# Two transformer layers on one core: where the second pass adds its third operand, and when five pieces of side work run

## The chip, the cores and the metric

The kernel runs on one core of a Trainium2 chip. A core has five engines, each with its own queue of instructions that it works off in order: TensorE (PE in the profile; its weight loads are PEld), VectorE (DVE), ScalarE (ACT), GpSimd (POOL) and SyncE (SP), which here only issues transfers. POOL and ACT issue transfers too. Sixteen DMA engines carry them all. The metric is the time of one execution on the device, in microseconds (us); lower is better.

## The reference, cut to what matters

The input is 8 sequences of 256 tokens with 512 features, in fp32. The reference runs two layers.

```python
x = x + L0_attn(layernorm(x)) + L0_ffn(layernorm(x))
x = x + L1_attn(layernorm(x)) + L1_ffn(layernorm(x))
```

`L0_attn` has 32 heads of 128. It takes queries, keys and values as `silu(xn @ qkv_w.T)`, weighs query-key scores with a decay instead of a softmax, multiplies them with the values, normalises over all heads, multiplies with `sigmoid(xn @ gate_w.T)` and projects back to 512 features. `L0_ffn` is a mixture of 16 experts, of which each token takes two, and a shared expert:

```python
y = y + ge[:, None] * ((silu(xt @ w1 + b1) * (xt @ w2 + b2)) @ w3 + b3)
```

`L1_attn` is one head of softmax attention of width 128. `L1_ffn` holds 64 pairs of low-rank factors, of which each token takes 16 by a softmax over its best scores:

```python
h = einsum("nd,krd->nkr", x, A); out = einsum("nkr,kdr->nd", h * G[:, :, None], B) * 2
```

## The kernel before, in words

**Tokens and stages.** The 2048 tokens are four chunks of 512. An opening (to about 130 us) normalises them, routes them to experts and runs the shared expert. Then come two passes over the heads of the first layer: the first takes chunks 0 and 1 together, the second chunks 2 and 3. Then the second layer takes the chunks one after another, 0 to 3 (from about 2420 us).

**Seven products for eight.** Large matrix products are made by a scheme that replaces eight half-size products by seven and some additions of halves, and this twice, one inside the other. A pass is 8 groups of four heads, each in two halves (`h`: first queries and keys, then gates and values), so 16 halves a pass, numbered through as `at`, 0 to 31 (16 to 31 are the second pass). A half is seven *outer* products (class `Outer`, L1177), in the order p1 p2 p6 p5 p3 p7 p4. In the first pass the sums of weight halves that they need are made on VectorE and GpSimd and stored; the second pass loads them.

An outer product is again seven *inner* products, each a few matmuls into a bank of 512 columns, in the order p1, p7, p3 of the outer product before, p6, p4, p2, p5. Three banks are read in between, while TensorE goes on: p1 fills bank `a` and it is copied to `c1`; p7 fills bank `e`, copied to `c3`; p6 adds onto `a`, copied to `c2`. The copies are ScalarE's (`copied`, L1199; the instruction is listed at L1201). TensorE may not add onto a bank until its copy is done: p6 waits for `c1`, p5 for `c2`, p4 for `c3`. Each of the four quarters of the result is a bank plus such a copy (`result`, L1204), an add on VectorE. What the outer scheme still wants is a third operand: the quarter of an earlier outer product (tile `a` or `c`), added by GpSimd in a second instruction, either in place (p2, p5, p3) or through a tile `r` (p6, p4, p7). One quarter, (0,1), takes no copy.

**The order of the rest.** Within the two passes the order on ScalarE, GpSimd and VectorE is that in which the program issues the instructions. After each inner product, `slot` (L881) takes the side work that is due, one counted piece at a time (two when more than twelve wait): `later(n, f)` (L877) makes `f` due n slots on. A half has 49 slots. Side work is:

- the attention of the head pairs and its results `gT`; `output` (L1039) makes from four of them the seven operands of the output projection, with adds and subtractions on GpSimd, and puts off each `project` (L1065) by some slots: p7 by 6;
- 36 expert tiles in the halves 17 to 27 (`expert`, L1296): two gathers on GpSimd's queue fetch tokens and weights into one of two large buffers, `staged`; 10 slots later the tokens are turned, 12 slots later a third gather puts the output bias where the tokens were (`bias`, L916), at 14 comes the first product, at 19 the second (`down`, L940), whose VectorE add reads that bias (`ye`);
- `low_sums` (L1351) for the two low-rank factors, in half 28 at slots 16 and 48: it loads quarters of a factor into the two `staged` buffers by SyncE, makes sums on GpSimd and stores them;
- `settle_early` (L1399), in half 29 at slot 34: loads chunk 1, gathers its two expert rows a token (`gather`, L614, eight gathers on GpSimd's queue), adds them times their gates (`settle`, L624, eight VectorE instructions), and stores the chunk;
- `wrapped_up` (L1405), in half 30 at slot 26: the same for chunk 0, and its normalisation. Both take the `staged` buffers as well.

**The second layer.** For each chunk, `seven` (L1533) runs three times: twice over the first low-rank factor (`low_rank`, banks times gates that are spread by DMA, `spread_g`) and once over the second. Lists of functions, `fill1` and `fill2`, are called after the named inner product. The operands of the second factor come by `load_fb` (L1600), called after p5 of the first `seven` of chunk 0. At the start of a chunk the next one is loaded (`next_x`); from chunk 1 on its expert rows are gathered into two `spare` buffers and settled inside the fills. Chunk 1 itself was settled before. Outside the two passes a scheduler arranges the order from these calls.

Of the kernel before, what the change touches and what calls it, by code (L numbers as in the profile page):

```python
# [24 lines left out]
NB = 2  # L25
# [4 lines left out]
NG = H // HG  # L30
# [43 lines left out]
def block_kernel(  # L74
# [721 lines left out]
    with tc.tile_pool(name="attn", bufs=1) as attn, tc.manual_schedule(engines={mybir.EngineType.Activation, mybir.EngineType.Pool, mybir.EngineType.DVE}):  # L796
# [232 lines left out]
        class Unit:  # L1029
# [9 lines left out]
            def output(self, l, t, pair, gT):  # L1039
# [7 lines left out]
                elif (t, pair) == (1, 0):  # L1047
                    O[l, "p7"] = self.gated()
                    sub(O[l, "p7"], A[l, 0, 0], gT, pool)
                    ready = (("p7", 6),)  # L1050
                elif (t, pair) == (1, 1):
                    O[l, "p4"] = gT
                    O[l, "p5"], O[l, "p6"] = A[l, 1, 0], A[l, 0, 0]
                    add(A[l, 1, 0], A[l, 1, 0], gT, pool)
                    sub(A[l, 0, 0], A[l, 1, 0], A[l, 0, 0], pool)
                    ready = (("p4", 3), ("p5", 7), ("p6", 10))
                else:
                    O[l, "p2"] = gT
                    O[l, "p3"] = A[l, 1, 1]
                    sub(A[l, 1, 1], gT, O[l, "p6"], pool)  # L1060
                    ready = (("p2", 4), ("p3", 7))
# [115 lines left out]
        class Outer:  # L1177
# [20 lines left out]

            def copied(self, bank):  # L1199
                c = attn.tile([P, 512], FP, tag="cp", name="cp", bufs=5)  # L1200
                nc.scalar.copy(c, bank)  # L1201
                return c

            def result(self, i, j, bank, c):  # L1204
# [7 lines left out]
                if made:  # L1212
# [5 lines left out]
                    else:  # L1218
                        add(o, bank, c)
                        if with_:  # L1220
                            add(o, o, u.tile(self.h, with_)[:, q], pool)
                elif c is None and p != "p7":
                    add(a, bank, a)
                else:
# [22 lines left out]
            def p1(self):  # L1247
                self.a = ps_a()
                self.go(self.a, "p1", True)
                self.c1 = self.copied(self.a)  # L1250
                self.after("p1")

            def p7(self):
                self.e = ps_e()
                self.go(self.e, "p7", True)
                self.c3 = self.copied(self.e)
                self.after("p7")

            def p6(self):
                self.go(self.a, "p6")  # L1260
                self.c2 = self.copied(self.a)
                self.after("p6")
# [33 lines left out]
        def expert(j):  # L1296
# [3 lines left out]
            later(14, e.up)  # L1300
            later(19, e.down)

# [95 lines left out]

        def settle_early():  # L1399

            x_, y = spare8(), spare8()
            settled_in(1, x_, y)
            later(41, lambda: nc.sync.dma_start(out=xs_[1], in_=x_))

        def wrapped_up():  # L1405
# [73 lines left out]
        for n, (i, g, h, p) in enumerate(plan):  # L1479
# [4 lines left out]
            if k == 0:  # L1484
# [12 lines left out]
                if at == 2 * NB * NG - 4:  # L1497
                    later(16, partial(low_sums, 0))
                    later(48, partial(low_sums, 1))
                if at == 2 * NB * NG - 2:  # L1500
                    later(26, wrapped_up)
                if at == 2 * NB * NG - 3:
                    later(34, settle_early)
            if h == 0 and k in (0, 2):
# [110 lines left out]
    for i in range(NCH):  # L1615
# [85 lines left out]
        if i + 1 < NCH:  # L1701
            following = [next_x(i + 1)]
            if i:
                following += [spare(), spare()]
                for n in range(TOP):
                    gather(i + 1, n, following[1 + n])
        fill1 = {
# [5 lines left out]
        if following:  # L1713
# [9 lines left out]
            if i:  # L1723
                fill1[1].append(lambda: finish(i + 1, following[0], kept=tc.keep_in_program_order))
            for n, fill, k, ts in () if i == 0 else (
                (0, fill1, 5, (0, 1)), (0, fill1, 3, (2, 3)), (1, fill1, 4, (0, 1)), (1, fill2, 2, (2, 3)),
            ):
# [5 lines left out]
        if i == 0:  # L1733
            fill1[5].append(load_fb)
        low_rank(0, fill1)
# [133 lines left out]
```

## Time and profile before

| what | value |
|---|---|
| median of 3 runs | 2734.82 us (2734.21 to 2735.54) |
| the profiled execution | 2731.75 us, span 2730.0 us |
| TensorE matmul busy | 2647.9 us (97%) |
| VectorE busy | 1759.5 us (64%) |
| GpSimd busy | 1655.1 us (61%) |
| ScalarE busy | 966.8 us (35%) |
| mean granted TensorE clock | 0.987 |

The span runs from the first instruction to the last. A matmul row is counted as busy while its columns stream, so a busy TensorE also includes time at a lower granted clock (PEclk, 1.00 is full speed). A line of waits reads: engine, tile and line that waited, what ended the wait, total us, how often, the longest. A line of the timeline reads: start, duration, engine, line, operation, output and inputs, form, how many were merged, and in brackets the idle time before it and what ended it. A line of windows gives a stretch, its length, and for each engine busy us and instructions, then PEclk, the busy share of the DMA engines and GB/s.

### The profile page before, as it was taken

How to read it: one execution, taken by the hardware profiler on the slowest of the kernel's cores; microseconds unless marked ns; L12 is line 12 of the kernel's file. 1: busy time of each engine (PE TensorE's matmuls, PEld its weight loads, DVE VectorE, ACT ScalarE, POOL GpSimd, SP SyncE). 2: the span in 40 equal slices, each digit the busy share in tenths (PEclk: the TensorE clock that was granted, in tenths of full speed). 3: DMA queues.
4: the chain of work that ended last, by engine and by line, in shares of the span. 5: the costliest groups of instructions: out<-in, count | busy, mean ns of one | idle time of the engine just before them, and what ended most of it. 6: DMA issues, size and time to landing. Idle time of an engine off the chain costs nothing. (4 is left out here: it accounts for less than half of the span.)

```text
span 2730.0 us, 39198 instructions
## 1 busy us (share of the span) xinstructions
PE 2647.9 (97%) x14218; PEld 2303.0 (84%) x14218; DVE 1759.5 (64%) x2985; ACT 966.8 (35%) x1455; POOL 1655.1 (61%) x1502
## 2 busy tenths in 40 slices
PE   8999999999999999999999999999999989999999
PEld 5488989898989898988889898888889878877777
DVE  8697777777778787856445454555555545756664
ACT  4234343433333334343434242333334232421121
POOL 7468686867686767667646556575746675662210
PEclk9999999999999999999999999999999999999999
DMA  6897777776777786867767676767677695632211
GB/s 247 305 380 284 262 263 274 256 284 244 284 256 284 264 287 239 300 250 272 251 231 279 226 273 222 278 229 271 248 247 260 233 336 197 225 98 104 80 49 64
DMA packets 163411, 657.74 MB, mean 241 GB/s; under 512 B 19808, under 2 KB 22368, under 8 KB 160992
## 3 DMA queue, kind: packets, MB, share of 16 engines
q1 hardware_dynamic: 126224, 501.26, 52.3%
q10 hardware_dynamic: 21024, 92.81, 8.4%
q0 software_dynamic: 15968, 61.13, 6.9%
q8 instruction: 115, 1.88, 0.3%
q14 instruction: 80, 0.66, 0.1%
HBM read 513.18 MB, written 144.83 MB: 241 GB/s over the span
## 5 line engine op out<-in xcount | busy, mean ns | idle before, releaser
L872 PE MATMUL ps_a<-xt,w 128*128 128x256 f32 x2688 | 720.9, 383 | 13.4 <-DMA xt<-xc 4.0
L1201 ACT COPY cp<-ps_a 128x512 f32<-128x512 f32 x448 | 261.5, 584 | 914.6 <-PE ps_a L872 820.8
L103 POOL TENSOR_TENSOR c<-c 128x512 f32<-128x512 f32 x288 | 374.0, 1311 | 332.5 <-DVE c L103 321.6
L103 POOL TENSOR_TENSOR c<-c,r 128x512 f32<-128x512 f32 x320 | 431.1, 1363 | 196.4 <-DVE r L103 178.9
L872 PEld LDWEIGHTS ps_a<-xt,w 128*128 128x128 f32 x2688 | 474.8, 193 | 69.6 <-issue 16.1
L1069 PE MATMUL ps_sc<-wo,gT 128*128 128x256 f32 x1792 | 427.1, 382 | 12.4 <-POOL gT L103 12.1
L1069 PEld LDWEIGHTS ps_sc<-wo,gT 128*128 128x128 f32 x1792 | 335.9, 191 | 58.0 <-POOL gT L103 13.6
L872 PE MATMUL ps_e<-xt,w 128*128 128x256 f32 x1344 | 369.9, 385 | 11.2 <-DVE c L103 9.6
L103 DVE TENSOR_TENSOR w<-w 128x256 f32<-128x256 f32 (+1 forms) x464 | 329.7, 720 | 9.0 <-DMA w<-in_w_att_dram 3.6
L103 POOL TENSOR_TENSOR sums<-sums,sq 128x256 f32<-128x256 f32 x240 | 193.3, 805 | 165.5 <-ACT sq L1007 155.9
L872 PEld LDWEIGHTS ps_a<-w,xt 128*128 128x128 f32 x1792 | 271.7, 192 | 23.5
L872 PE MATMUL ps_a<-w,xt 128*128 128x128 f32 x1792 | 273.2, 275 | 0.0
L872 PEld LDWEIGHTS ps_e<-xt,w 128*128 128x128 f32 x1344 | 234.4, 193 | 37.1 <-DVE c L103 11.7
L103 DVE TENSOR_TENSOR acc<-ps_sc,acc 128x512 f32<-128x512 f32 x196 | 134.9, 688 | 188.4 <-PE ps_sc L1069 188.2
L1016 DVE SCALAR_TENSOR_TENSOR gT<-ps_o,nw,c 128x256 f32<-128x256 f32 x256 | 111.9, 478 | 206.7 <-ACT sq L1007 202.4
L1201 ACT COPY cp<-ps_e 128x512 f32<-128x512 f32 x224 | 131.2, 586 | 192.1 <-PE ps_e L872 188.2
L103 DVE TENSOR_TENSOR s<-ps_sc,decay 128x384 f32<-128x384 f32 x256 | 139.6, 551 | 78.9 <-PE ps_sc L984 77.8
L872 PE MATMUL ps_b<-xt,w 128*128 128x256 f32 x672 | 182.1, 380 | 0.0
L103 DVE TENSOR_TENSOR c<-ps_a,c 128x512 f32<-128x512 f32 x160 | 109.9, 687 | 102.9 <-PE ps_a L872 101.3
L103 DVE TENSOR_TENSOR c<-c,r 128x512 f32<-128x512 f32 x128 | 174.7, 1395 | 0.1
L103 POOL TENSOR_TENSOR gT<-gT 128x512 f32<-128x512 f32 x128 | 166.7, 1302 | 2.9 <-DVE gT L1016 0.4
L996 PE MATMUL ps_o<-s,c 128*128 128x256 f32 x512 | 156.7, 388 | 7.2 <-DVE gT L1016 6.3
(289 smaller groups left out, 4208.9 us busy)
## 6 DMA issues: line engine op xcount, KB each, us to landing
xt<-xc SPq DMA_DIRECT2D x224, 896.0 KB
w<-in_w_att_dram SPq DMA_DIRECT2D x144, 512.0 KB
w<-in_w_att_dram SPq DMA_DIRECT2D x48, 384.0 KB
wo<-in_w_out_dram SPq DMA_DIRECT2D x56, 256.0 KB
decay<-dec SPq DMA_DIRECT2D x32, 384.0 KB
yd<-ye SPq DMA_DIRECT2D x36, 256.0 KB
wos<-wo ACTq DMA_DIRECT2D x32, 256.0 KB
wo<-wos SPq DMA_DIRECT2D x32, 256.0 KB
```

What stands on the lines that cost most here:

```text
L103: (eng or nc.vector).tensor_tensor(o, a, b, op)
L872: mm(o, a, b, start=(first and ty == 0), stop=True, skip_group_check=True)
L996: mm(po[:, bass.ts(hh, S)], v[:, 0:P], s[:, 0:S], start=True, stop=False)
L1016: nc.vector.scalar_tensor_tensor(gT[:, h, :], po[:, bass.ts(h, S)], nw[:, n : n + 1], self.c[:, 2 * h + t, 0:S], ALU.mult, ALU.mult,)
L1069: mm(py[:, bass.ts(t, S)], self.O[l, p][:, hh, bass.ts(t, P)], self.wo[p][:, hh, :], start=(t == 0 and hh == 0), stop=(hh == 1), skip_grou ...
L1201: nc.scalar.copy(c, bank)
```

## The change

In the second pass, thirteen of the copies of a half's outer products (all three of p2, p6, p5 and p3, and `c2` of p4) become a VectorE add of the bank and the third operand. The later add of bank and `c` then yields the whole result, and GpSimd's add is left out. Five pieces of side work move: the projection p7 from 6 to 8 slots (both passes), `down` from 19 to 24, the second `low_sums` from slot 48 to 57; `settle_early` is gone, and chunk 1 is gathered and settled in the second layer, in the fills of chunk 0; `load_fb` is called after p2 of the second `seven` instead of after p5 of the first. The calls that settle in the fills move by some products in all chunks.

```diff
-                    ready = (("p7", 6),)
+                    ready = (("p7", 8),)
...
-            def copied(self, bank):
+            def folded(self, q):
+
+                return self.u.i and (self.p, q) not in (("p4", 0), ("p4", 3)) and {"p2": "a", "p5": "a", "p6": "a", "p4": "a", "p3": "c"}.get(self.p)
+
+            def copied(self, bank, q):
                 c = attn.tile([P, 512], FP, tag="cp", name="cp", bufs=5)
-                nc.scalar.copy(c, bank)
+                with_ = self.folded(q)
+                if with_:
+                    add(c, bank, self.u.tile(self.h, with_)[:, q])
+                else:
+                    nc.scalar.copy(c, bank)
                 return c
...
                         add(o, bank, c)
-                        if with_:
+                        if with_ and not self.folded(q):
                             add(o, o, u.tile(self.h, with_)[:, q], pool)
-                elif c is None and p != "p7":
-                    add(a, bank, a)
+                elif p != "p7" and (c is None or self.folded(q)):
+                    add(a, bank, a if c is None else c)
                 else:
...
-                self.c1 = self.copied(self.a)
+                self.c1 = self.copied(self.a, 0)
...
-            later(19, e.down)
+            later(24, e.down)
...
-        def settle_early():
-
-            x_, y = spare8(), spare8()
-            settled_in(1, x_, y)
-            later(41, lambda: nc.sync.dma_start(out=xs_[1], in_=x_))
...
-                    later(48, partial(low_sums, 1))
+                    later(57, partial(low_sums, 1))
...
-                if at == 2 * NB * NG - 3:
-                    later(34, settle_early)
...
-            following = [next_x(i + 1)]
-            if i:
-                following += [spare(), spare()]
-                for n in range(TOP):
-                    gather(i + 1, n, following[1 + n])
+            following = [next_x(i + 1), spare(), spare()]
+            for n in range(TOP):
+                gather(i + 1, n, following[1 + n])
...
-            for n, fill, k, ts in () if i == 0 else (
-                (0, fill1, 5, (0, 1)), (0, fill1, 3, (2, 3)), (1, fill1, 4, (0, 1)), (1, fill2, 2, (2, 3)),
+            for n, fill, k, ts in (
+                (0, fill1, 3, (0, 1)), (0, fill1, 4, (2, 3)), (1, fill2, 2, (0, 1)), (1, fill2, 7, (2, 3)),
             ):
...
         if i == 0:
-            fill1[5].append(load_fb)
+            fill2[2].append(load_fb)
```

More of the change, by code (lines that the diff above doesn't have):

```diff
@@ L1255, in p7 @@
                 self.go(self.e, "p7", True)
-                self.c3 = self.copied(self.e)
+                self.c3 = self.copied(self.e, 3)
                 self.after("p7")
@@ L1260, in p6 @@
                 self.go(self.a, "p6")
-                self.c2 = self.copied(self.a)
+                self.c2 = self.copied(self.a, 2)
                 self.after("p6")
```

## The prediction

> **What bounds the kernel now.** I read the page first: TensorE is busy 97% of the span, so only its remaining idle time, and time at a lowered clock, can be won. I then asked who TensorE waited for, by stage, then for the clock around each long wait, and last for the timeline ahead of them, to see what held the engine that was late.
>
> Waits of TensorE, first pass (130 to 1230 us) and second (1230 to 2420):
>
> ```profile
> PE ps_sc L1069 <- POOL gT L103: 12.1, 8, 2.2
> ...
> PE ps_e L872 <- DVE c L103: 9.6, 3, 3.4
> PE ps_o L996 <- DVE gT L1016: 5.4, 1, 5.4
> PE ps_sc L983 <- ACT c L960: 4.7, 3, 3.1
> PE ps_a L872 <- DMA xt<-xc: 4.0, 1, 4.0
> PE ps_a L872 <- DVE c L103: 2.8, 1, 2.8
> PE ps_a L872 <- DVE r L103: 2.2, 2, 1.2
> ```
>
> Few and long waits, not many short ones. Windows of 15 us around five of the longest and around one at 630 us:
>
> ```profile
> 1390.00:1405.00 15.00, 11.64 (x48) 9.63 (x48) 5.25 (x8) 3.66 (x5) 7.88 (x7) 0.77 0.67 230
> 1550.00:1565.00 15.00, 11.82 (x57) 10.07 (x56) 6.46 (x11) 4.02 (x6) 9.23 (x9) 0.89 0.76 265
> 2192.00:2207.00 15.00, 10.97 (x56) 9.87 (x55) 4.08 (x7) 3.34 (x5) 11.45 (x11) 0.77 1.02 393
> 2244.00:2259.00 15.00, 9.57 (x38) 8.17 (x37) 6.35 (x9) 8.83 (x11) 12.26 (x12) 0.77 0.44 161
> 2312.00:2327.00 15.00, 11.77 (x44) 9.26 (x43) 9.58 (x11) 4.36 (x7) 13.08 (x11) 0.77 0.89 333
> 625.00:640.00 15.00, 12.83 (x72) 11.33 (x72) 11.23 (x16) 4.72 (x7) 11.32 (x11) 0.89 0.68 222
> ```
>
> The third column from the end is PEclk: each long wait is followed by a stretch at lowered clock that costs (1 - 0.77) x 15 = 3.45 us or (1 - 0.89) x 15 = 1.65 us more. What comes before the wait at 1395, and before that at 2198 (timeline):
>
> ```profile
> 1387.37 1.02 POOL L918 DMA_INDIRECT xw<-in_b_dram,own__1114  x1 [0.16 <-PE ps_a L872]
> 1394.38 0.69 DVE L103 TENSOR_TENSOR ye<-ps_sc,xw 128x512 f32<-128x512 f32 x1 [6.46 <-DMA xw<-in_b_dram,own__1114]
> 1395.73 2.07 PE L872 MATMUL ps_e<-xt,w 128*128 128x256 f32 x4 [3.36 <-DVE c L103]
> ...
> 2181.66 8.00 SPq L1364 DMA_DIRECT2D low<-in_fb_dram  x3
> ```
>
> The bias of an expert is fetched at 1387.37 and VectorE stands 6.46 us at the add that reads it; the banks queue behind. SyncE stands 8.00 us at the second factor's loads, until the first factor's buffers are stored, and TensorE then lacks tokens for 4.0 us.
>
> **The change, part by part.**
>
> *p7 two slots later.* All eight waits of 12.1 us are p7's operand, made by GpSimd, in the first pass. In the built order the projection now stands behind two more inner products, which start 0.88 us apart there: 1.76 us of cover. The four waits of 2.15 to 2.19 us keep 0.4 each, the rest go; the lowered clock at 630 us (1.65) goes too. 12.1 - 1.6 + 1.65 = **-12.1**. The seven `gT` buffers are held two products longer; no wait of the trace is for one of them, so I charge nothing. If the cover fails, 12.1 stays.
>
> *`down` five slots later.* The waits of 9.6 us (1395, 1554, 1712) all follow a `ye` that stood 6.2 to 6.5 us for its bias. Five slots are at least 5 x 0.86 (the spacing of inner products in the other halves) = 4.3 us and with the slots' own matmuls more like 7; GpSimd, rid of its adds, also fetches sooner. **-9.6 - 3.45 - 1.65 - 1.65 = -16.35.** Late next: in the three halves with four experts the gather for the second next expert stands ahead of `down` in the built order and now waits on GpSimd's queue for that `ye`, a slot or two; behind it stand the next bias (eleven slots of cover) and sums. Nothing for it in the sum.
>
> *Second factor nine slots later.* Nine slots are over 7.7 us, and SyncE stood 8.00; GpSimd reaches the stores sooner. **-4.0 - 3.45 = -7.45.**
>
> *Chunk 1 leaves the second pass.* At 2250 TensorE waits 5.4 us for `gT`, after GpSimd did four gathers and the adds queued behind them, on which ScalarE's gates (7.87 us) and the queue behind hung. At 2316 GpSimd had stood 6.9 us for the store of `settle_early`'s buffer before `wrapped_up` could gather. Both causes go: **-5.4 - 3.45 - 2.8 - 3.45 = -15.1.** Two 1 MB loads or stores on SyncE's queue and eight gathers (1.05 us each) go with it.
>
> *Third operand on VectorE.* 16 halves x 13 = 208 copies (ScalarE, 584 ns) become VectorE adds. The new form (bank and tile) has its row: c<-ps_a,c, 689 ns. So VectorE gets 208 x 0.689 = 143 us: 636 of 1190 us busy becomes 779 (65%). GpSimd loses 208 adds of 1.28 to 1.33 us, some 270 of 728 us. These rows of the second pass carry it:
>
> ```profile
> L103 DVE TENSOR_TENSOR c<-c,r 128x512 f32<-128x512 f32 x64 | 87.4, 1397 | 0.1
> L103 DVE TENSOR_TENSOR c<-ps_a,c 128x512 f32<-128x512 f32 x78 | 53.8, 689 | 64.4 <-PE ps_a L872 62.8
> L103 POOL TENSOR_TENSOR c<-c 128x512 f32<-128x512 f32 x141 | 178.3, 1280 | 188.5 <-DVE c L103 185.5 <-DVE rms L244 2.4
> ```
>
> Gained: silu and gate no longer wait for GpSimd to finish a tile, so the 4.7 us before L983 go, with the clock after the first (1.65): **-6.35**. Paid: TensorE needs a copied bank again two inner products later. At 0.86 us each that is 1.7 us, against 0.69 plus some 0.25 to hand over. What matters is whether VectorE is free. I laid the 208 adds into its queue in the timeline, each behind what the program issues before it: seven in ten start as the bank is ready, and all but 16 end before TensorE needs the bank. The 16 are late by 20.1 us together; 8.6 of that are two places (1252, 2171) where VectorE sits in c<-c,r rows of up to 5.4 us while GpSimd runs the adds that go. From 0 to +20; I take **+8**, near the 11.5 left without those two.
>
> *Layer 2, chunk 0.* Eight VectorE settles (0.74 us in the quiet rows, 1.12 in the second pass: 6 to 9 us) and eight gathers come in. GpSimd runs the gathers ahead of four bias adds, which end near 2460 instead of 2452.6; VectorE wants the first at 2463.7, so that hides. The gathers move 2.1 MB while the DMA engines are full (2450 to 2465, 254 to 399 GB/s): 6.7 us more ahead of the first `spread_g`, on which VectorE already stood 7.5 and 3.3 us and TensorE 2.2. In the other direction, in SyncE's built order the first transfer of the second factor stays put, and its other four (2.1 MB) now follow the second `spread_g`, on which VectorE stood 5.2 us and TensorE later 1.8 and 4.2. Ends: +6.7 and a lowered clock, and two microseconds for the settles, +12; or -6. I take **+4**, since the settles must end before the statistics that TensorE's 4.2 us hang on.
>
> *Moved settles of chunks 2 and 3*: TensorE has only 1.4 and 0.75 us waits there; nothing.
>
> Sum: -12.1 - 16.35 - 7.45 - 15.1 - 6.35 + 8 + 4 = **-45.4**. Against the profiled execution, 2731.75, that is 2686.4; that execution was 3.1 us under the median 2734.8, so on the median **2689**.
>
> A rule weighed against the rows: the Trainium skill (TensorE: Matmul & The Clock Gate, Part 1) lets the clock fall after an idle window of some 3.4 us. By it the waits of 2.2, 2.8, 3.05, 3.15, 3.2 and 3.36 us would not lower the clock, and the sum would lack 1.65 + 3.45 + 1.65 + 1.65 + 1.65 + 3.45 = 13.5 us, for 2703. PEclk shows 0.77 and 0.89 behind just these waits, so the rows decide. Another (SBUF: State Buffer, Who interferes with whom) says that a VectorE instruction with one SBUF input does not meet GpSimd, one with two does; by that rule, the trace agrees: 689 ns throughout for c<-ps_a,c, 1397 on average for c<-c,r. It changes no term.
>
> **The rivals.**
>
> *VectorE becomes the bound (slower).* In the p4 products of halves with gates, six copies came out 0.8 us late in my laying. If one copy in each of the 80 outer products were so late, that is 64 us: 2734.8 - 53.4 + 64 = 2745 (53.4 is the sum without the +8). It outweighs the gain from 0.26 us a copy. For it: VectorE works in order, and stood 120 us for `gT` in this pass. Against: those stands end when TensorE gets there, so no bank is waiting yet; median cover left is 2 us.
>
> *Waits move on.* GpSimd and VectorE stall elsewhere, as a stall's end only uncovers the next: half of the second pass's 45.2 us comes back: 2689 + 22.6 = 2712. For it: the gathers that wait for `ye`, and 2.2 us at 2334 and 2358 behind settles. Against: GpSimd falls to near 40% busy.
>
> *Better.* With GpSimd's adds gone, c<-c,r (1397 ns, 0.69 us in its quiet rows) gets shorter, the late copies vanish (-8) and layer 2 gives -6: 2689 - 18 = 2671.
>
> *The retimings do nothing and the copies cost little*: within 0.2% (5.5 us, about what a measurement here can tell from no change). This needs every long wait to come back.
>
> **How the numbers follow.** My forecast, 2675 to 2705: 0.57. Better: 0.07. Waits move on, 2705 to 2729: 0.23. No change: 0.04. Slower: 0.09. Faster is 0.57 + 0.07 + 0.23 = 0.87. The range 2668 to 2722 leaves out the last two, about 0.05 of the moved waits and 0.02 below.
>
> **What would show it.** In the changed kernel's waits: L1069 <- gT below 2 us in the first pass; no `ye` <- DMA row; no SyncE stand at L1364; no wait over 3 us between 1230 and 2420, PEclk 1.00 there; VectorE near 65%, GpSimd near 38% in that stretch. I am wrong if TensorE shows many short waits ps_a <- DVE cp (VectorE the bound), if long waits stand at other places, or if 2440 to 2500 grows by more than 12 us.

## The result, and the profile after

| | before | after |
|---|---|---|
| median, same chip, five executions each | 2734.21 us | 2720.82 us |
| ratio | | 0.9952, 95% interval 0.9938 to 0.9967 |
| profiled execution | 2731.75 us | 2719.83 us |
| first pass (from about 130 us to the end of its last outer product), us | 1051.5 | 1059.0 |
| second pass, us | 1210.6 | 1186.3 |
| turn to layer 2 and its chunk 0, us | 128.8 | 132.9 |
| layer 2, chunk 1, us | 74.6 | 73.7 |

The change is 13.4 us (0.5%) faster, where 45.4 were forecast. The second pass is 24.3 us shorter; the first pass (7.5 longer) and the turn to layer 2 (4.1 longer) give part of that back. The stretches of the table are cut at the same TensorE instructions in both traces.

TensorE's waits after, first pass (130 to 1230 us). The columns are engine, tile and line that waited, what ended the wait, total us, how often, the longest:

```profile
PE ps_o L996 <- DVE gT L1016: 8.5, 8, 1.4
```

and second pass (1230 to 2420):

```profile
PE ps_sc L983 <- DVE s L103: 6.0, 3, 2.5
PE ps_sc L912 <- DMA xw<-xnd,whose: 5.3, 2, 5.0
PE ps_sc L1069 <- DVE gT L1016: 3.0, 1, 3.0
```

Three things stand in these rows. The 12.1 us that `L1069` waited for p7's operand are gone from the first pass, and in their place TensorE waits for VectorE (8.5 us here, and 6.5 us of `L872` for VectorE's `c`). TensorE's waits behind the expert's bias, the silu waits, the wait for the second factor and the one at 2316 are gone from the second pass. And three waits are new there: for the scores `s` of VectorE, for an expert's tokens at 1284, and 3.0 for `gT` at 2237 where 5.4 stood at 2250.

Busy us by windows (length, then PE, PEld, DVE, ACT, POOL, then PEclk, DMA share, GB/s) show that the load moved as worked out:

```profile
1230.00:2420.00 1190.00, 1169.87 (x6660) 1041.62 (x6659) 775.25 (x1224) 321.07 (x451) 474.31 (x447) 1.00 0.69 245
```

VectorE is at 775 / 1190 = 65% (65 forecast), GpSimd at 40% (38 forecast), and no wait of TensorE for a copied bank (`cp`) is longer than 0.6 us in this pass. The groups of the second pass (line, engine, operation, tiles, shape, count, then busy us and mean ns of one, then the idle time before them) show the adds that replace the copies (140 of them here, on bank `a`; 62 more on bank `e`), at the 689 ns that was taken for them, and VectorE's add of two SBUF tiles, which was 1397 ns before and is no shorter:

```profile
L103 DVE TENSOR_TENSOR cp<-ps_a,c 128x512 f32<-128x512 f32 x140 | 96.3, 688 | 33.0 <-PE ps_a L872 29.6 <-PEq L1319 1.6 <-issue 0.3
L103 DVE TENSOR_TENSOR c<-c,r 128x512 f32<-128x512 f32 x64 | 92.9, 1484 | 4.9 <-ACT r L1235 4.9
```

In layer 2 the timeline (start, duration, instruction, idle before it) shows a new long wait:

```profile
2448.26 0.69 DVE L103 TENSOR_TENSOR hg<-cp,spread_g 128x512 f32<-128x512 f32 x1 [15.55 <-DMA spread_g<-gd]
...
2449.61 2.93 PE L1652 MATMUL ps_e<-t,fa 128*128 128x256 f32 x6 [10.01 <-DVE cp L103]
```

VectorE stands 15.55 us for the first `spread_g`, which was 7.54 us before, with TensorE behind it.

### The profile page after: what moved, and what is told of

Its sections match the earlier page's. It is cut to its first block, busy times and chain, and to the rows that moved or that the text cites. A ratio compares the mean times of both kernels' runs of the same rounds, so it can differ in the third digit from the quotient of the medians.

```text
span 2718.1 us, 38734 instructions
## 1 busy us (share of the span) xinstructions
PE 2637.7 (97%) x14218; PEld 2296.1 (84%) x14218; DVE 1915.6 (70%) x3193; ACT 850.6 (31%) x1249; POOL 1401.4 (52%) x1294
## 5 line engine op out<-in xcount | busy, mean ns | idle before, releaser
L872 PE MATMUL ps_a<-xt,w 128*128 128x256 f32 x2688 | 718.5, 382 | 9.9 <-ACT cp L1209 4.0
L872 PEld LDWEIGHTS ps_a<-xt,w 128*128 128x128 f32 x2688 | 470.8, 191 | 67.2 <-issue 10.3
L103 POOL TENSOR_TENSOR c<-c,r 128x512 f32<-128x512 f32 x256 | 352.8, 1393 | 239.9 <-DVE r L103 220.7
L1069 PE MATMUL ps_sc<-wo,gT 128*128 128x256 f32 x1792 | 424.2, 380 | 4.5 <-DVE gT L1016 3.0
L1209 ACT COPY cp<-ps_a 128x512 f32<-128x512 f32 x304 | 177.5, 584 | 676.5 <-PE ps_a L872 582.5
L1069 PEld LDWEIGHTS ps_sc<-wo,gT 128*128 128x128 f32 x1792 | 335.2, 191 | 49.5 <-DVE gT L1016 3.5
L872 PE MATMUL ps_e<-xt,w 128*128 128x256 f32 x1344 | 366.7, 382 | 6.5 <-DVE c L103 6.5
L103 DVE TENSOR_TENSOR w<-w 128x256 f32<-128x256 f32 (+1 forms) x464 | 353.0, 769 | 5.4
L872 PEld LDWEIGHTS ps_a<-w,xt 128*128 128x128 f32 x1792 | 270.5, 191 | 23.0
L872 PE MATMUL ps_a<-w,xt 128*128 128x128 f32 x1792 | 272.2, 274 | 0.0
L103 POOL TENSOR_TENSOR c<-c 128x512 f32<-128x512 f32 x144 | 191.4, 1340 | 146.5 <-DVE c L103 138.2
L872 PEld LDWEIGHTS ps_e<-xt,w 128*128 128x128 f32 x1344 | 232.8, 192 | 32.5 <-DVE c L103 8.0
L872 PE MATMUL ps_b<-xt,w 128*128 128x256 f32 x672 | 182.6, 380 | 0.0
L1007 ACT ACTIVATE sq<-ps_o 128x512 f32<-128x512 f32 x128 | 76.6, 599 | 285.3 <-PE ps_o L997 260.7
L996 PE MATMUL ps_o<-s,c 128*128 128x256 f32 x512 | 157.3, 389 | 8.8 <-DVE gT L1016 8.5
```

The costliest lines, as they stand in the source:

```text
L103: (eng or nc.vector).tensor_tensor(o, a, b, op)
L872: mm(o, a, b, start=(first and ty == 0), stop=True, skip_group_check=True)
L996: mm(po[:, bass.ts(hh, S)], v[:, 0:P], s[:, 0:S], start=True, stop=False)
L1007: nc.scalar.activation(sq, po, AF.Square)
L1069: mm(py[:, bass.ts(t, S)], self.O[l, p][:, hh, bass.ts(t, P)], self.wo[p][:, hh, :], start=(t == 0 and hh == 0), stop=(hh == 1), skip_grou ...
```

## The experiments

All were timed beside the kernel before on the same chip; across the runs that kernel's medians lie between 2732.3 and 2734.2 us, so times of different runs can be set side by side to about 2 us.

| kernel | median us | ratio to before, 95% interval |
|---|---|---|
| the change | 2720.8 | 0.9952 (0.9938 to 0.9967) |
| before + the fold alone | 2707.1 | 0.9907 (0.9892 to 0.9923) |
| before, GpSimd's 208 adds left out | 2706.6 | 0.9898 (0.9883 to 0.9913) |
| after without the fold | 2730.2 | 0.9986 (0.9977 to 0.9995) |
| before + p7 at 8 | 2746.2 | 1.0040 (1.0027 to 1.0053) |
| after with p7 at 6 | 2709.9 | 0.9917 (0.9903 to 0.9930) |
| before, p7's difference left out | 2729.0 | 0.9981 (0.9970 to 0.9992) |
| before + `down` at 24 | 2728.7 | 0.9984 (0.9975 to 0.9993) |
| after with `down` at 19 | 2706.6 | 0.9905 (0.9890 to 0.9920) |
| after with `down` at 22 | 2707.0 | 0.9905 (0.9889 to 0.9919) |
| after with `down` at 23 | 2706.7 | 0.9899 (0.9885 to 0.9913) |
| after, GpSimd's adds of p7's `r` left out | 2699.6 | 0.9880 (0.9859 to 0.9901) |
| before + chunk 1 in layer 2, second factor later | 2718.6 | 0.9944 (0.9931 to 0.9957) |
| after with chunk 1 settled early | 2721.6 | 0.9964 (0.9951 to 0.9976) |
| after, first spread ahead of the gathers | 2720.1 | 0.9957 (0.9942 to 0.9973) |
| **after with p7 at 6 and `down` at 19** | **2696.1** | **0.9864 (0.9850 to 0.9879)** |
| the same with p7 at 7 | 2697.8 | 0.9868 (0.9854 to 0.9882) |
| the same (p7 at 6), first spread and settles moved | 2700.4 | 0.9880 (0.9865 to 0.9895) |

### What the fold is worth

The change without its fold:

```diff
-                with_ = self.folded(q)
-                if with_:
-                    add(c, bank, self.u.tile(self.h, with_)[:, q])
-                else:
-                    nc.scalar.copy(c, bank)
+                nc.scalar.copy(c, bank)
...
-                        if with_ and not self.folded(q):
+                        if with_:
                             add(o, o, u.tile(self.h, with_)[:, q], pool)
-                elif p != "p7" and (c is None or self.folded(q)):
-                    add(a, bank, a if c is None else c)
+                elif c is None and p != "p7":
+                    add(a, bank, a)
```

> The kernel after with ScalarE's copies and GpSimd's adds as before; everything that was moved stays moved. By the prediction's terms the fold is worth -6.35 + 8, about nothing: 2717 to 2723, with waits of L983 for ScalarE's c (4.7 us) back in the second pass. Rival one (the fold carries the second pass's gain, since without it GpSimd is late for the gathers and the sums): second pass from 1186 to 1200 or more, time over 2732. Rival two (the fold costs: the 6.0 us that L983 waits for VectorE's s come from it): second pass 1180, time 2712 to 2716.

Measured: 2730.2 us, 9.4 more than the change, second pass 1201.8 us. The first rival was nearest: the fold carries 15.5 of the 24.3 us that the second pass wins, though the time stayed 2 us under this rival's 2732. So the fold alone was put into the kernel before, with the same lines the other way round:

> The kernel before with the thirteen adds of the bank and the third operand alone; nothing moved in time. The prediction's terms (silu waits -6.35, late copies +8): 2735 within 3. Rival, from the run without them (2730.2 against 2720.8): GpSimd is what the long waits of the second pass hang on, and taking 208 adds from it shortens most of them; the ye waits (9.6 us) and the gT wait (5.4 us) of TensorE fall to half or less, second pass 1194 to 1200 instead of 1210.6, time 2717 to 2724.

Measured: 2707.1 us, 25 less than before and 13.7 less than the whole change. The five moves, taken together, cost time. The second pass is 1184.7 us. What happened to the late bias is seen in two lines of its timeline, beside those of before (bias fetched at 1387.37, `ye` at 1394.38 after 6.46 us):

```profile
1380.19 1.00 POOL L918 DMA_INDIRECT xw<-in_b_dram,own__1114  x1 [2.36 <-PE ps_sc L912]
...
1391.48 0.69 DVE L103 TENSOR_TENSOR ye<-ps_sc,xw 128x512 f32<-128x512 f32 x1 [0.17 <-PE ps_sc L942]
```

With its adds gone, GpSimd waits for the tokens to be turned and fetches the bias 9.7 us earlier, counted from TensorE's turning of these tokens (1379.32 here, 1376.80 before), with `down` still at slot 19. `ye` waits 0.17 us, for its own product. The fold alone thus does what `down` was moved for. For the bias it was order more than load: in the kernel before, GpSimd stood idle at the first of three adds that lie ahead of the bias in its queue, until VectorE had made the tile that it adds to:

```profile
1380.72 1.27 POOL L103 TENSOR_TENSOR c<-c 128x512 f32<-128x512 f32 x1 [7.52 <-DVE c L103]
```

Is it GpSimd that is emptied, or ScalarE, or the shorter path? The kernel before, with the 208 adds simply left out (`folded` as in the change) and the copies left with ScalarE:

```diff
                         add(o, bank, c)
-                        if with_:
+                        if with_ and not self.folded(q):
                             add(o, o, u.tile(self.h, with_)[:, q], pool)
-                elif c is None and p != "p7":
-                    add(a, bank, a)
+                elif p != "p7" and (c is None or self.folded(q)):
+                    add(a, bank, a if c is None else c)
```

> The kernel before with GpSimd's 208 adds of the third operand in the second pass left out and nothing put in their place (ScalarE copies as before, VectorE adds nothing more; that operand is missing from the result). First theory (the long waits of the second pass hang on GpSimd, and the fold gains by emptying it): as fast as the fold alone, 2707, or faster by what VectorE's 208 adds cost; second pass 1175 to 1186. Rival (the fold gains by taking the copies from ScalarE or by shortening the path to the gates): no more than a third of the fold's 25 us, 2725 or above. The difference to the fold alone is the price of the adds on VectorE, for which the prediction took +8.

Measured: 2706.6 us, second pass 1183.5. All of the fold's 25 us are there without any work for VectorE and with ScalarE's copies kept, so neither of these carries the gain: what counts is that the adds leave GpSimd. Whether an emptied queue or a shorter path to each tile did it, the run can't tell by itself, since with the add left out a tile is ready sooner too. At two places the traces speak for the queue: the fetch of the bias reads no such tile, and around the silu wait at 1259 GpSimd of the kernel before ran adds without a gap from 1239.5 to 1262.5, where with the 208 adds left out it stood idle 11.1 us up to 1249.0. How the whole gain splits is not shown. The 208 adds on VectorE, 143 us of its time by the prediction's estimate, cost 0.6 us with overlapping intervals, so nothing that can be measured.

### p7 later

```diff
-                    ready = (("p7", 8),)
+                    ready = (("p7", 6),)
```

> The kernel after, with p7 back at 6 slots. First theory (the stall only moved: in these halves VectorE's queue sets the pace, and the two slots put it further behind TensorE): the first pass goes back from 1059 to about 1051 us, the eight waits of L1069 for gT (12.1 us) return, and the waits for gT of L1016, c and r (8.5 + 6.5 + 1.5 us) go; time 2721 - 7.5 = 2713, 2711 to 2716. Rival, the prediction's own reason (p7 later wins 12.1): 2733. Second rival (the two first passes differ by chance from one execution to the next): 2721 within 2.

Measured: 2709.9 us, 11 less; the first pass is 1054.2 us with the eight waits of `L1069` back at 12.0 us. The first theory holds in sign, and VectorE's waits of `L996` and of `L872` for `c` fall to 1.0 and 0.6 us; but the gain is larger than its 7.5 us and lies elsewhere in part: 4.8 us in the first pass, in these two traces 2.4 in the second and 4.0 in the turn to layer 2. To see what the wait itself is worth, the kernel before with GpSimd's subtraction left out:

```diff
-                    O[l, "p7"] = self.gated()
-                    sub(O[l, "p7"], A[l, 0, 0], gT, pool)
+                    if self.i:
+                        O[l, "p7"] = self.gated()
+                        sub(O[l, "p7"], A[l, 0, 0], gT, pool)
+                    else:
+                        O[l, "p7"] = gT
```

> The kernel before, in which the first pass multiplies by gT itself in the place of p7's difference: GpSimd's subtraction (16 in the first pass) is left out, so that part of the result is not computed; p7 stays at 6 slots. First theory (VectorE's queue sets the pace): L1069 waits no more for gT, but as much comes back as waits for VectorE's gT, c and r; first pass 1048 to 1054 us (before 1051.5), time 2730 to 2737. Rival (GpSimd's late difference is what costs, and the two slots did other harm): first pass 1039 us, 12 less, and 2722 within 3.

Measured: 2729.0 us, 1 us under the first theory's range and 7 over the rival's 2722; first pass 1048.4, 3.1 less. TensorE's waits there, 130 to 1230 us:

```profile
PE ps_o L996 <- DVE gT L1016: 8.7, 8, 1.4
...
PE ps_a L872 <- DVE r L103: 2.6, 4, 0.6
```

where the first row of the kernel before was

```profile
PE ps_o L996 <- DVE gT L1016: 0.9, 2, 0.5
```

With nothing of p7's left to wait for, TensorE runs into VectorE some products later: 7.8 us more of waits for `gT` and 2.6 new ones for `r` stand against the 12.1, and its idle time in this pass falls from 18.5 to 15.9 us only. The wait at `L1069` was time in which VectorE caught up. Then p7 at 8 alone, and at 7 in the fastest kernel:

```diff
-                    ready = (("p7", 6),)
+                    ready = (("p7", 8),)
```

> The kernel before with p7 at 8 alone. The prediction's term: 2722. Theory (VectorE's queue sets the pace of these halves, and with p7 later TensorE runs into it with waits for gT, c and r): L1069's waits for gT gone in the first pass, waits of L996 for gT (8 us) and of L872 for c (6 us) in their place, 2736 to 2745. Rival (p7's loss came only beside the fold): 2733.

> The fastest kernel so far (2696) with p7 at 7. If the loss lies in the second slot only (the inner product before which p7 then stands): 2694 to 2698, and L1069's waits for gT half as long. If each of the two slots costs: 2701 to 2703.

Measured: 2746.2 us for 8 alone, 12.5 slower than before and 1 over the theory's range; 2697.8 for 7, 1.7 over 6 with overlapping intervals. Waits of p7 at 8 alone, first pass:

```profile
PE ps_o L996 <- DVE gT L1016: 8.5, 8, 1.4
PE ps_e L872 <- DVE c L103: 6.7, 9, 1.2
```

and in the second pass

```profile
PE ps_sc L912 <- DMA xw<-xnd,whose: 4.1, 1, 4.1
```

Over all kernels here the first pass took 1057.0 us on average with p7 at 8 (nine traces, 1055.5 to 1059.0) and 1053.0 with p7 at 6 (eight traces, 1051.5 to 1054.2). So p7 at 8 costs 4 us there, not -12.1. The rest of its loss is in the second pass, where a wait of 3.8 to 5.0 us for an expert's tokens stands at about 1280 us in each of the nine traces, with a stretch of 3.4 or 6.8 us at half speed; with p7 at 6 it is at most 1.9 us. The pairs of traces do not agree on the whole loss there (2.4 us in the change, 7.1 with `down` at 19, 12.6 in the kernel before). In the trace of p7 at 8 alone the gather of these tokens stands on GpSimd until a store of the first pass's results has landed, where it stood 2.05 us in the kernel before:

```profile
1278.70 1.06 POOL L898 DMA_INDIRECT xw<-xnd,whose  x1 [6.44 <-DMA xs<-spare]
```

With p7 at 7 the wait for tokens is 1.1 us, the first pass takes 1054.3 us and `L1069` waits 5.1 us where it waited 12.0, as the reading of a loss in the second slot alone asked; why the gather is in time at 7 and not at 8 was not taken further.

### `down` later

```diff
-            later(19, e.down)
+            later(24, e.down)
```

> The kernel before with down at 24 alone. The prediction's term (-16.35): 2717 within 3, the three waits of ps_e for c (9.6 us) gone and nothing in their place. Rival (GpSimd is the late engine and down only decides who stands for it): the waits come back as L912 for the tokens' gather (8.6 us in the run without the fold) or L983 for VectorE's s (6.0 us), second pass 1205 to 1212, time 2726 to 2734.

Measured, in the kernel before: 2728.7 us, 3.7 less. The rival holds: the bias waits of 9.6 us go, and waits for `s` take their place:

```profile
PE ps_sc L983 <- DVE s L103: 6.5, 3, 2.4
```

```diff
-            later(24, e.down)
+            later(19, e.down)
```

> The kernel after with down back at 19 (p7 stays at 8). If the prediction's term holds beside the fold: the ye waits return, +16, 2737. Rival one (a GpSimd with 208 adds fewer fetches the bias in time, so down's place is worth little): 2718 to 2724. Rival two (the waits of L983 for s, 6.0 us, and L912 for the gather, 5.3 us and 3.4 us of clock, are down's own doing): these go and nothing returns, 2708 to 2714.

Measured, in the change: 2706.6 us, 14 less. Rival two is nearest: no wait of `L983` is left, and no bias wait comes back. Of its other row, `L912`, 3.8 us stay; that is the wait for tokens of p7 at 8 (above).

The suspect was GpSimd's queue: in halves of four experts the gather for the second next expert stands ahead of the `down` that frees its buffer. In the built order this is so at 24 and at 23, and no more at 22:

```diff
-            later(24, e.down)
+            later(22, e.down)
```

> The kernel after with down at 22: GpSimd's built order has the bias and the adds ahead of the gather again in the halves of four experts. Theory (the gather that stands for the ye two experts before holds up GpSimd's adds, which then run beside VectorE's and make s late): L983's three waits for s (6.0 us) are gone, time 2707 to 2711, as with down at 19. Rival (each slot of delay costs alike): about two fifths of the 14 us, 2715.

```diff
-            later(24, e.down)
+            later(23, e.down)
```

> The kernel after with down at 23: GpSimd's built order is as at 24. Theory of the queue: the three waits for s stay, 4 to 6 us, time 2718 to 2721. Rival (delay alone): a fifth of the 14 us, 2718, with waits a fifth shorter; taken with slot 22 a straight line is the rival, a step between 22 and 23 the theory.

Measured: 2707.0 and 2706.7 us. There is a step, as the theory of the queue asked, but between 23 and 24, where GpSimd's order is the same. That theory fell, and so did the one of delay alone. The timelines show what differs. After, with `down` at 24 (GpSimd, VectorE and TensorE put together in order of time):

```profile
1411.01 1.00 POOL L898 DMA_INDIRECT xw<-xnd,whose  x1 [8.38 <-DVE r L103]
...
1413.94 6.78 DVE L103 TENSOR_TENSOR c<-c,r 128x512 f32<-128x512 f32 x2
...
1414.63 4.93 POOL L103 TENSOR_TENSOR c<-c,r 128x512 f32<-128x512 f32 x4
...
1420.64 0.54 DVE L103 TENSOR_TENSOR s<-ps_sc,decay 128x384 f32<-128x384 f32 x1
...
1421.24 0.70 PE L983 MATMUL ps_sc<-c 128*128 128x256 f32 x2 [2.52 <-DVE s L103]
```

With `down` at 23:

```profile
1406.03 1.00 POOL L898 DMA_INDIRECT xw<-xnd,whose  x1 [8.18 <-DVE xeT L914]
...
1409.67 3.71 POOL L103 TENSOR_TENSOR c<-c,r 128x512 f32<-128x512 f32 x3
...
1410.67 3.87 DVE L103 TENSOR_TENSOR c<-c,r 128x512 f32<-128x512 f32 x2
1414.46 0.55 DVE L103 TENSOR_TENSOR s<-ps_sc,decay 128x384 f32<-128x384 f32 x1
```

GpSimd stands about 8 us for the buffer in both. But p7's quarters `r` are each added twice, to one tile by GpSimd and to another by VectorE, and at 24 GpSimd comes free just as VectorE begins its add: the four adds that had queued up run without a gap, and VectorE's stands until they are through. Durations of that add (min, median, max in ns) around the three late `s`, from three windows:

```profile
L103 DVE TENSOR_TENSOR c<-c,r x2: 677/3426/6174, 1413.9 to 1420.0; 128x512 f32<-128x512 f32 x2
L103 DVE TENSOR_TENSOR c<-c,r x3: 674/1746/4141, 1569.3 to 1575.5; 128x512 f32<-128x512 f32 x3
L103 DVE TENSOR_TENSOR c<-c,r x3: 676/1746/4506, 1723.7 to 1730.3; 128x512 f32<-128x512 f32 x3
```

An instruction of 0.67 us took 6.17, 4.14 and 4.51 us in the second pass just there. In all six kernels with `down` at 24 that keep GpSimd's adds, with the fold or without it, one such add stands 4.0 to 6.2 us at each of these three places; in the eleven with `down` at 19 or 22 none there takes over 3 us, and at 23 one of the three does (3.26 us). To see whether this collision is the cause, GpSimd's adds of `r` were taken away, with `down` still at 24:

```diff
-                        add(c_, c_, r, pool)
+                        if not u.i:
+                            add(c_, c_, r, pool)
```

> The kernel after, down still at 24, with GpSimd's four adds of p7's r to the tile c left out in the second pass (64 adds; that product is missing from the gates and values); VectorE's adds of the same r to the tile a stay, and so do all slots. Theory (collision: VectorE's add stands until GpSimd's burst ends): no c<-c,r on VectorE over 2 us, the three waits of L983 for s (6.0 us) gone, second pass 1172 to 1181, time 2704 to 2711. Rival (VectorE's own order at slot 24 makes s late): the three waits stay, 4 us or more, time 2716 or above.

Measured: 2699.6 us, second pass 1170.4, and no wait of `L983`. The same row over the second pass (1230 to 2390 us):

```profile
L103 DVE TENSOR_TENSOR c<-c,r x64: 674/684/1755, 1254.5 to 2351.9; 128x512 f32<-128x512 f32 x64
```

The collision makes `s` late. The run is faster than expected. One part of that can be read: the 3.0 us that `L1069` waited for `gT` at 2237 in the change are gone too, and they stood behind an add of the same kind that took 5.35 us (from 2231.3) beside three of GpSimd's. What else the 64 adds fewer on GpSimd are worth is not separated. Neither part says anything of slot 24. One point stays open: of the 14 us between 24 and 23, the two profiled executions differ by 11.0, of which 6.4 lie in the second pass, 2.4 in the turn to layer 2 and 2.3 in the first pass, which `down` does not touch. In the pair with p7 at 6 (`down` at 24 and at 19) the second pass differs by 11.2: 6.5 us of waits for `s` and, behind two of the three, lowered clock.

### Chunk 1 and the second factor

The moves of chunk 1, `load_fb` and the second factor's sums alone, in the kernel before:

```diff
-                    later(48, partial(low_sums, 1))
+                    later(57, partial(low_sums, 1))
...
-                if at == 2 * NB * NG - 3:
-                    later(34, settle_early)
...
-            following = [next_x(i + 1)]
-            if i:
-                following += [spare(), spare()]
-                for n in range(TOP):
-                    gather(i + 1, n, following[1 + n])
+            following = [next_x(i + 1), spare(), spare()]
+            for n in range(TOP):
+                gather(i + 1, n, following[1 + n])
...
-            fill1[5].append(load_fb)
+            fill2[2].append(load_fb)
```

> The kernel before with chunk 1 settled in the second layer, load_fb late and the second low_sums at slot 57; no fold, p7 at 6, down at 19. The prediction's terms: -15.1 - 7.45 + 4 = -18.6, 2714 within 4. Rival (the wait for gT at 2250 is not chunk 1's doing, since it is there in the run without the fold as well, 6.0 us, and layer 2 pays): second pass 10 us shorter at most, chunk 0 of layer 2 4 to 7 longer, time 2724 to 2731.

Measured: 2718.6 us, 15.4 less, where -18.6 was the forecast of these three terms (the calls that settle in the fills move with them, for all chunks). The second pass is 1197.0 us, 13.6 less; a wait of 3.5 us for `gT` stays of the 5.4. The other way round, chunk 1 early again in the change (its `settle_early` and the settles of the later chunks go back too):

```diff
...
-                    later(57, partial(low_sums, 1))
+                    later(48, partial(low_sums, 1))
...
+                if at == 2 * NB * NG - 3:
+                    later(34, settle_early)
...
-            following = [next_x(i + 1), spare(), spare()]
+            following = [next_x(i + 1)]
+            if i:
+                following += [spare(), spare()]
...
```

> The kernel after with chunk 1 settled in the second pass as before (and so the second low_sums back at slot 48, since both want the same buffers); load_fb stays late, p7 at 8. By the prediction's terms (-7.45 - 15.1 + 4 undone): 2721 + 18.5 = 2739. Rival (the stalls at 2198, 2250 and 2316 came from a full GpSimd, which the fold has emptied): they come back at a third or less, and layer 2's chunk 0 gets 4 to 12 us shorter since no gathers stand ahead of its spread: 2712 to 2721.

Measured: 2721.6 us, no difference that can be told: the second pass is 11.5 us longer, the turn with chunk 0 7.2 shorter and the first pass, which the edit does not touch, 2.3 shorter. In the second pass the move is worth nearly what it was in the kernel before (13.6): without it the wait for `gT` is 6.0 us again, and only the wait for tokens of the second factor stays small (0.5). So the rival's reason, a GpSimd that the fold has emptied, does not hold there, though its time was near. The fold alone had left the longest of these waits as well, in its second pass:

```profile
PE ps_o L996 <- DVE gT L1016: 6.1, 1, 6.1
```

and with the moves of this section on top of the fold the time falls from 2707.1 to 2696.1 us ("A faster kernel", below). What differs is the price at the turn: with the move it is 0.3 us longer in the kernel before, 2.7 shorter beside the fold, and 7.2 longer in the change. Over all traces but those of the two runs below that rearrange layer 2, the turn took 130.5 us with chunk 1 in layer 2 (ten traces, 128.9 to 133.0) and 128.4 without (seven, 125.8 to 131.9), the stage of chunk 1 72.7 and 74.1, and what follows, to TensorE's last instruction, 130.6 and 129.4. So layer 2 pays about 2 us on average, within the scatter of single traces; why the turn is so long in the change stays open.

Can the late first spread be won back? Its four transfers were issued on GpSimd's queue ahead of chunk 1's gathers:

```diff
...
+        early = []
+        if i == 0:
+            early = [spread(h * HJ, nc.gpsimd) for h in range(2)]
...
```

> The kernel after, with the first four transfers of the spread gates of chunk 0 in the second layer issued on GpSimd's queue ahead of chunk 1's eight gathers. First theory (the first spread lands late, 2448 us, because the gathers were put ahead of it): VectorE's wait for spread_g falls from 15.55 us to under 8, TensorE's wait of 10.0 us at 2449 to under 3 and the 5.1 us of lowered clock go; chunk 0's stage 133 to about 121, time 2709 within 4. Rival (the transfer engines are full there in any case, with the factors' loads): the spread or the settles stay late, gain under 4, 2717 to 2721.

Measured: 2720.1 us (2714.0 to 2725.8), the rival. The spread comes sooner, and VectorE stands at the settles instead, for rows that now land later:

```profile
2434.12 0.69 DVE L103 TENSOR_TENSOR hg<-cp,spread_g 128x512 f32<-128x512 f32 x1 [7.52 <-DMA spread_g<-gd]
...
2444.08 7.74 DVE L629 SCALAR_TENSOR_TENSOR spare<-spare,slot_gates 128x512 f32<-128x512 f32 x2
...
2452.48 3.78 PE L1653 MATMUL ps_e<-yT,fa 128*128 128x256 f32 x8 [6.43 <-DVE cp L103]
```

### A faster kernel

Without the two moves that cost:

```diff
-                    ready = (("p7", 8),)
+                    ready = (("p7", 6),)
...
-            later(24, e.down)
+            later(19, e.down)
```

> The kernel after with p7 back at 6 and down back at 19: the fold and chunk 1's move alone. If the two losses (11 and 14 us, each undone alone) are apart from one another: 2696, 2693 to 2700, no wait of L983 for s. Rival (they share a part, since both move work in the second pass): 2701 to 2707, no better than either alone.

Measured: 2696.1 us, 38 under the kernel before and 25 under the change: the two losses (11 and 14) add up. TensorE's longest waits in its second pass (1230 to 2420), where 5.4 us was the longest before:

```profile
PE ps_sc L1069 <- DVE gT L1016: 2.5, 1, 2.5
PE ps_a L872 <- DVE cp L103: 2.2, 1, 2.2
```

The first stands behind the same kind of collision: VectorE's add of `c` and `r` took 5.37 us from 2210.8. That pass takes 1172.6 us, 38 less than before, which is what the prediction's terms for it came to (37.25), reached with other parts. And on top of it the spread's transfers moved as above, with chunk 1's settles in the second `seven` (for chunk 1 alone; its statistics move back by a product or so too):

```diff
...
-                (0, fill1, 3, (0, 1)), (0, fill1, 4, (2, 3)), (1, fill2, 2, (0, 1)), (1, fill2, 7, (2, 3)),
+                (0, fill2, 2, (0, 1)), (0, fill2, 7, (2, 3)), (1, fill2, 5, (0, 1)), (1, fill2, 5, (2, 3)),
...
```

> As the run before, and in layer 2's chunk 0 the first four spread transfers on GpSimd's queue ahead of chunk 1's gathers, and chunk 1's eight settles moved into the second seven, behind the first low-rank half, so that VectorE does not stand at them. Theory (in the run with the transfers moved alone, VectorE stood in the settles for 7.7 us instead, since the gathers had not landed): chunk 0's stage falls from 129 to 133 us to under 122, time 8 to 12 under the run before. Rival (the statistics then come too late for the next chunk, or the transfers are bound by their volume): gain under 4 us, the wait at the turn to chunk 1.

Measured: 2700.4 us, 4 slower; the turn with chunk 0 took 132.4 us, and the theory falls. What bounds that stretch was not taken further.

## Why the prediction was right and wrong

**Right.** The sign, and the range of 2668 to 2722, though the time lies at its edge and the gain of 13.4 us is less than a third of the 45.4 forecast. It lies in the rival "waits move on" (2712), which had 0.23. VectorE did not become the bound: its load is the one worked out, and the price of the copies, set at +8 from 0 to +20, is 0.6. The bias, silu and second-factor waits went. The terms for chunk 1 and the second factor were nearly right: -18.6 forecast together, -15.4 measured alone and -11 beside the fold, nearly all in the second pass; the +4 for layer 2 came out as 4.1 in the change's trace, but it lies within the scatter of other traces, so that is luck as much as reckoning. (The 8.00 us at SyncE is the length of three issues; the wait in it was 6.7.)

**Wrong, the term for p7 (-12.1).** "In the built order the projection now stands behind two more inner products ... 1.76 us of cover." The cover was there, and `L1069` stopped waiting. But the step took TensorE's wait for lost time, and looked only at what it waits for. The run without the subtraction shows that only 3.1 us of the 12.1 were won in this pass: VectorE is as late as GpSimd, some products on. Two slots on, the first pass is 4 us longer and a wait for tokens opens in the second; the term is +12.5 alone and +11 inside the change. The rival of a wait that moves on was held against the second pass only.

**Wrong, the term for `down` (-16.35).** The waits for `ye` do go. But they go with the fold alone, so the change could not win them a second time: the terms of the fold and of `down` were summed as if they were apart, although the step itself said that GpSimd, rid of its adds, also fetches sooner. And "Late next ... Nothing for it in the sum" is where the price lay: GpSimd stood for the `ye`, as that sentence said, and then ran its adds in a burst against VectorE's. Measured: -3.7 in the kernel before, where the bias waits could still be won, and +14 beside the fold, where only the burst is left.

**Wrong, the fold (+1.65, from -6.35 and +8).** It is -25. The prediction counted the silu waits alone for GpSimd's 270 us less of adds, and booked the bias waits to `down`. Taken at the prediction's own sizes, these two, 6.35 and 16.35, make 22.7 us, and the fold alone shortens the second pass by 25.9. That GpSimd's queue was behind both could be read in the rows of before: a bias fetched behind three adds, gates late by GpSimd's adds. The wait for `gT` at 2250 is another matter: the fold leaves it (6.1 us).

**The rule on VectorE and GpSimd.** The prediction cited the Trainium skill (SBUF: State Buffer, Who interferes with whom), by which a VectorE instruction with two SBUF inputs meets GpSimd, and said that it changes no term. The trace agrees with the rule (0.67 us quiet, 6.17 us beside four adds of GpSimd), but it did change a term: that of `down`. The prediction had seen rows of up to 5.4 us at two places, but put them down to the adds that go; GpSimd's adds of `r` stay, and they make the bursts.

**The sum.** Four runs lead from the kernel before to the change, one part at a time; each step is a difference of ratios times 2733 us. The fold: -25.4 (0.9907). Chunk 1 with the second factor on top: -11.8 (0.9864). `down` at 24 on top: +14.5 (0.9917). p7 at 8 on top: +9.6 (0.9952). Together -13.1. Alone in the kernel before, the same parts are worth -25.4, -15.3, -4.4 and +10.9: `down` depends most on what else is there.

## What to carry to other kernels

When several waits stand behind the queue of one engine, cost the edit that empties this queue first, and cost every other edit on the trace that would then be left; here the fold did the work of `down` as well and left `down` only its harm. Before a wait is booked as gain, ask which other engine is as late a few instructions on: leave out what is waited for in one run, and see how much of the wait is really won. A small delay of side work should be tried at several values, since its price can be a step (23 slots or 24 here), not a slope.

## What was not expected of the hardware

**A VectorE add of two SBUF tiles can stand for a whole burst of GpSimd adds, not for one.** With 128x512 fp32 tiles it took 0.67 us alone, about 1.75 us beside a single GpSimd add (which then took 1.64 to 1.78 us, and 1.25 to 1.28 in a burst), and 6.17 us where four followed one another without a gap, ending 0.55 us after the last. With GpSimd's adds of the same `r` gone, the median over the second pass fell from 1.55 to 0.68 us and the longest from 6.17 to 1.76. It is not so each time: beside other bursts it slipped in between two adds.

**The same wait lowers the clock in one execution and not in the next.** In the first pass with p7 at 6, waits of 2.14 to 2.19 us recur at about 362, 496, 630 and 765 us. In the profiled execution of before only the third was followed by a half-speed stretch (3.4 us long); in six other traces it was the second and the fourth, and in a seventh the third again. All half-speed stretches within the two passes lasted 3.4, 6.8 or 10.2 us. After a wait of 3.01 us (2237, after) none followed. By the Trainium skill (TensorE: Matmul & The Clock Gate, Part 1) the clock falls after an idle window of some 3.4 us; these rows are all below it, so the trace differs from the rule there, and 1.65 or 3.45 us a wait can only be booked as a chance.
